# Three sequences in one expert table, the fourth through all experts: a routed block on one core

## The chip, the cores and the metric

The kernel runs on one core of a Trainium2 chip. The metric is the device time of one execution in microseconds (us). The engines are named as in the profile: PE (TensorE matmuls; PEld its weight loads), DVE (VectorE), ACT (ScalarE), POOL (GpSimd) and SP (SyncE, which here only issues DMAs). Each engine runs its own instructions in the order in which they were laid down.

## The reference

The input is four sequences (b = 0 to 3) of 512 tokens with 128 features. A modulated layer norm, a convolution block with a gate and a residual come first, per sequence. Then each token goes to 8 of 160 small experts:

```python
logits = x @ router_w.T + expert_bias[None, :]
probs = jax.nn.sigmoid(logits)
top_w, top_idx = jax.lax.top_k(probs, TOP_K)
top_w = top_w / (jnp.sum(top_w, axis=-1, keepdims=True) + 1e-09)
top_w = top_w * ROUTED_SCALE
combine = combine.at[jnp.arange(T)[:, None], top_idx].set(top_w)
h1 = jax.nn.silu(jnp.einsum('th,eih->eti', x, w_gate))
h1w = h1 * combine.T[:, :, None]
routed = jnp.einsum('eti,ehi->th', h1w, w_down)
shared = jax.nn.silu(x @ w_gate_shared.T) @ w_down_shared.T
```

The output is x + gb * (routed + shared), where gb is a modulation per sequence. All is float32.

## The kernel before, in words

**Sequences.** `sequence(b)` (L281) is a generator with five parts; the loop at L954 interleaves the parts of neighbouring sequences. It computes the convolution block, the router's probabilities `prob` (L418), the 8 largest (`top`, L439), and from running counts a table row for each choice (`ranks`, `keys`, `slot_in`, L456 to L512). `shared` is the shared expert.

**Two halves.** Sequences 0 and 1 share one table and one pass of the experts, 2 and 3 another. A table has 64 rows for each expert and 56 (`NOV`, L50) spare blocks of 128 rows for experts that get more: 17,408 rows of 512 bytes. `clear(i)` (L149) writes zeros into a whole table beforehand, on SP's queue.

**Dispatch.** `dispatch(b)` (L627) scatters the tokens into the table: 32 indirect DMAs on POOL (L661), each after a small copy `pick` (L659). Between them it runs other POOL work, step by step: `residual_sums`, and `places(b)` (L592), which computes the weights of each choice.

**Experts.** `experts(s)` (L676) walks over its table in groups of 1,024 rows: 10 groups of own rows (`own_blocks`, 16 experts each, weights resident) and 7 of spare blocks (`overflow_blocks`, whose weights `ow` are loaded by 8 DMAs of SP, L740, at addresses that it reads at run time). A group is: load `xg` (L685), 8 transposes into `px` (L691), two copies to `xs` (L692), matmuls into `ph` (L714 or L750), Silu (L719 or L755), matmuls into `py` (L724 or L760), two copies to `yg` (L702, L703), and a store into the result table (L704). `xg`, `xs`, `yg` and `ow` have two buffers each.

**Combine.** `combine(b)` (L769) gathers the 8 result rows of each token: 32 indirect DMAs on POOL (L800). For b < 2, POOL also multiplies each gathered row by its weight (L777) and DVE adds up (L786); for b of 2 and 3, DVE does both (L782, L784).

**Fallback.** If the spare blocks don't suffice, `dense(b)` (L811) under `tc.If` (L981) computes a sequence through all 160 experts. In this data that branch isn't taken.

**Order.** Each buffer has a tag (`own(b, ...)`: one buffer for odd and one for even sequences; `bank(i, ...)`, `ps_x`, `ps_y`: two PSUM banks each). A planner lays down each engine's order ahead of the run, by the order of the program and by its own view of when things are ready; `behind(b, what)` pins an instruction behind another of its engine. The end of the program is:

```python
    dispatch(B - 1)
    for _ in places(B - 1, nc.vector):
        pass
    w_pairs += [weights(g) for g in (NGO - 2, NGO - 1)]
    experts(0)
    outs = [combine(b) for b in range(2)]
    experts(1)
    outs += [combine(b) for b in range(2, B)]
```

Of the kernel before, what the change touches and what calls it, by code (L numbers as in the profile page):

```python
# [39 lines left out]
P = 128  # L41
# [8 lines left out]
NOV = 56  # L50
# [42 lines left out]
def adaln_block(  # L93
# [48 lines left out]
    tables, results = [], []  # L142
    for i in range(2):
        t = dram.tile([ROWS, D], F32, tag=f"table{i}", name=f"table{i}")
        tables.append(t)
        t = dram.tile([ROWS, D], F32, tag=f"result{i}", name=f"result{i}")
        results.append(t)

    def clear(i):  # L149
        nc.sync.dma_start(  # L150
            tables[i].rearrange("(p i r) f -> p i (r f)", p=P, r=4),
            zero.unsqueeze(1).to_broadcast([P, ROWS // P // 4, 4 * D]),
        )

    clear(0)
    for b in range(2, B):
        nc.sync.dma_start(x_sb[b], rows_of(x_rows, b))
    clear(1)
# [30 lines left out]

    mark = const.tile([P, P], BF16, name="mark")  # L190
# [15 lines left out]
    short = const.tile([1, 2], I32, name="short")  # L206
# [69 lines left out]
    ready, halves, keep, last, scattered, residual, found, shared = ({} for _ in range(8))  # L276

    def behind(b, what):
        return tc.issue_after(last[what, b].ins) if (what, b) in last else nullcontext()

    def sequence(b):  # L281
# [153 lines left out]
        chosen = own(b, [P, NT, E], BF16, "out_wg", "chosen")  # L435
        for half in range(2):
            for t in (2 * half, 2 * half + 1):

                nc.vector.max(out=top[:, t, :], in_=prob[:, t, :])  # L439
                nc.vector.match_replace(  # L440
                    out=repl[:, t, :], in_to_replace=top[:, t, :], in_values=prob[:, t, :], imm_value=-1.0
                )
            at = ds(2 * half, 2)
            nc.vector.tensor_scalar(chosen[:, at, :], repl[:, at, :], 0.0, None, ALU.is_lt)
        h2 = own(b, [P, NT, D], F32, "h2", "h2")
# [15 lines left out]
        new, away = ranks[:, 4, :].bitcast(I32), ranks[:, 5 - b % 2, :]  # L461

        cum = ranks[:, 5, :] if b % 2 else own(b, [P, E], F32, "cum", "cum")
        if b % 2 == 0:
            nc.vector.tensor_single_scalar(new, n, P - 1.0 - BLK, ALU.add)
        else:
            was = halves[b // 2]
            nc.vector.scalar_tensor_tensor(new, n, P - 1.0 - BLK, was["cap"], ALU.add, ALU.subtract)
        nc.vector.tensor_single_scalar(new, new, 7, ALU.logical_shift_right)
        nc.vector.tensor_tensor_scan(  # L470
            cum, ones_e, new, 0.0 if b % 2 == 0 else was["cum"][:, E - 1 : E], ALU.mult, ALU.add
        )
        nc.vector.tensor_sub(away, cum, new)
        if b % 2:
            nc.vector.tensor_sub(away, away, was["new"])
        nc.vector.scalar_tensor_tensor(away, away, float(P), far, ALU.mult, ALU.add)
        if b % 2:
            nc.vector.tensor_sub(away, away, was["moved"])
        key_at = key_own if b % 2 == 0 else was["key"]
# [4 lines left out]
        for half in range(2):  # L484
# [15 lines left out]
            if b % 2 == 0:  # L500
                nc.vector.scalar_tensor_tensor(k1, rank, MARK + BLK, both(away), ALU.is_ge, ALU.mult)
            else:
                nc.vector.scalar_tensor_tensor(k1, rank, -MARK - BLK, both(was["cap"]), ALU.add, ALU.is_ge)
# [5 lines left out]
        ikey = work.tile([P, NT, TOPK], I32, tag="ikey", name=f"ikey{b}", bufs=B)  # L509
# [6 lines left out]
        with behind(b, "slots"):  # L516

            if b % 2 == 0:
                newf = own(b, [P, E], F32, "newf", "newf")
                nc.vector.tensor_copy(newf, new)  # L520
                moved = own(b, [P, E], F32, "moved", "moved")
                nc.vector.scalar_tensor_tensor(moved, newf, 1.0, away, ALU.is_ge, ALU.mult)
                cap = own(b, [P, E], F32, "cap", "cap")
                nc.vector.scalar_tensor_tensor(cap, newf, float(P), n, ALU.mult, ALU.subtract)
                key1 = own(b, [P, E], F32, "key1", "key1")
                nc.vector.tensor_add(key1, key_own, moved)
                nc.vector.tensor_add(key1, key1, n)
                halves[b // 2] = {"cap": cap, "cum": cum, "new": newf, "moved": moved, "key": key1}
            else:

                junk = ranks[0:NOV, 0, :]
                eo = own(b, [NOV, 2], F32, "eo", "eo")
                for i, c in enumerate((was["cum"], cum)):
                    nc.vector.scalar_tensor_tensor(
                        junk, c[0:NOV, :], iota_q[0:NOV], ones_e[0:NOV, :], ALU.is_le, ALU.mult,
                        accum_out=eo[:, i : i + 1],
                    )
                nc.vector.scalar_tensor_tensor(eo[:, 0:1], eo[:, 0:1], float(E), eo[:, 0:1], ALU.is_lt, ALU.mult)
                nc.vector.tensor_add(eo[:, 0:1], eo[:, 0:1], eo[:, 1:2])
                peo = bank(b, f"peo{b}")  # L540
                nc.tensor.matmul(peo[0:1, 0:NOV], eo[:, 0:1], ident[0:NOV, 0:NOV], start=True, stop=True)
                eo_row = work.tile([1, NOV], I32, tag="eo_row", name=f"eo_row{b}", bufs=2)
                nc.vector.tensor_scalar_min(eo_row, peo[0:1, 0:NOV], float(E - 1))
                nc.vector.tensor_single_scalar(
                    short[:, b // 2 : b // 2 + 1], cum[0:1, E - 1 : E], float(NOV), ALU.is_gt
                )
                halves[b // 2]["eo_row"] = eo_row
# [3 lines left out]
        row = work.tile([P, NT, TOPK], U32, tag="row", name=f"row{b}", bufs=B)  # L551
        idx = work.tile([P, NT, TOPK], U32, tag="idx", name=f"idx{b}", bufs=B)
# [5 lines left out]

        ph = bank(b, f"phs{b}")
# [209 lines left out]
    def combine(b):  # L769
# [37 lines left out]
        while pending:  # L807
            finish(*pending.pop(0))
# [241 lines left out]
```

## Time and profile before

| | us |
|---|---|
| median of 3 runs (lowest, highest) | 522.31 (520.89, 526.49) |
| the profiled execution: time | 523.86 |
| its span, first to last instruction | 522.2 |
| PE busy (2,532 matmuls) | 305.5 (59%) |
| POOL busy | 358.0 (69%) |
| DVE busy | 221.1 (42%) |
| ACT busy | 152.5 (29%) |
| moved by DMA | 98.57 MB |

Spans are counted from the first instruction. A PE that is busy need not be at its peak: matmuls are pipelined and their ends are modelled. A float32 matmul is two MATMUL records (two passes), a transpose or a bf16 matmul is one.

### The profile page before, as it was taken

Reading aid. Unit: us, or ns where it says so; the run is one execution under the profiler, and the core shown is the slowest. Engines: PE = TensorE matmul, PEld = TensorE weight load, DVE = VectorE, ACT = ScalarE, POOL = GpSimd, SP = SyncE. Lnnn points to the kernel's source line nnn. Section 1 sums busy time; section 2 is a strip of 40 time slices with the busy share of each in tenths; the row PEclk is TensorE's granted clock in tenths of the full one; section 3 lists DMA queues with packets and bytes.
Section 4 is the critical chain, followed back from the end, with each engine's and each line's share of the span. In section 5 each row is a group of like instructions: output and inputs, shape, how many; then the busy total and the mean of one; then the engine's idle time right before and its main releaser. Section 6 shows DMA issues by size and latency. Waiting matters only on the chain.

```text
span 522.2 us, 7733 instructions
## 1 busy us (share of the span) xinstructions
PE 305.5 (59%) x2532; PEld 208.2 (40%) x2532; DVE 221.1 (42%) x708; ACT 152.5 (29%) x298; POOL 358.0 (69%) x520
## 2 busy tenths in 40 slices
PE   5996997895569687676865834667777630000000
PEld 3644443443333466555643633545665520000000
DVE  7286785892586256562621401111332004333331
ACT  3463645351614152121210221314545520000000
POOL 8616168988888888568878038888898018777771
PEclk9999997798569997696885766657878985555555
DMA  8999994025411455395886583426999921212111
GB/s 273 409 394 409 324 419 196 30 80 153 137 35 66 146 185 176 118 288 170 284 291 212 184 260 126 167 82 211 300 302 299 335 103 45 70 50 75 50 56 36
DMA packets 50368, 98.57 MB, mean 189 GB/s; under 512 B 7633, under 2 KB 26130, under 8 KB 48914
## 3 DMA queue, kind: packets, MB, share of 16 engines
q1 hardware_dynamic: 36144, 61.20, 34.3%
q0 software_dynamic: 8192, 16.79, 10.4%
q10 hardware_dynamic: 5986, 20.03, 10.3%
q8 instruction: 22, 0.36, 0.3%
q14 instruction: 24, 0.20, 0.1%
HBM read 50.54 MB, written 47.45 MB: 188 GB/s over the span
## 4 chain that ended last, share of the span: by engine, by line
POOL 26%; PE 25%; issue 22%; DMA 10%; DVE 9%; ACT 3%; SPq 2%; POOLq 1%; ACTq 0%; DVEq 0%
POOL table L661 11%; POOL yk L800 10%; PE px L691 5%; PE py L724 4%; PE ph L714 4%; DMA xg<-table 3%; PE ph L750 2%; POOL pick L659 2%; PE py L760 2%; PE ph L323 2%; SPq L740 2%; DMA ow<-in_w_ov 2%; DMA yk<-result,row 2%; DMA mat<-in_mats 2%; DVE s L370 1%
## 5 line engine op out<-in xcount | busy, mean ns | idle before, releaser
L800 POOL DMA_INDIRECT yk<-result,row x128 | 124.9, 976 | 72.7 <-issue 51.8
L661 POOL DMA_INDIRECT table<-h,pick x116 | 118.8, 1024 | 33.5 <-POOL pick L659 17.5
L691 PE MATMUL px<-ident,xg 128*128 128x128 f32 x272 | 52.0, 337 | 26.3 <-issue 13.3
L691 PEld LDWEIGHTS px<-ident,xg 128*128 128x128 f32 x272 | 38.1, 171 | 34.7 <-issue 24.6
L724 PE MATMUL py<-w_g,h 64*64 64x128 f32 x640 | 32.1, 348 | 21.7 <-issue 16.2
L714 PE MATMUL ph<-xs,w_g 128*64 128x64 f32 x640 | 38.3, 262 | 9.6 <-issue 9.0
L784 DVE SCALAR_TENSOR_TENSOR out_sb<-yk,idx,out_sb 128x128 f32<-128x128 f32 x56 | 19.9, 355 | 48.9 <-DMA yk<-result,row 47.2
L659 POOL COPY pick<-slot_in 128x1 uint32<-128x1 uint32 x116 | 26.1, 226 | 19.9 <-DVE slot_in L512 19.5
L786 DVE TENSOR_TENSOR out_sb<-out_sb,yk 128x128 f32<-128x128 f32 x48 | 15.0, 319 | 57.1 <-POOL yk L777 47.6
L702 ACT COPY yg<-py 128x512 f32<-128x512 f32 x34 | 19.9, 585 | 65.9 <-PE py L724 21.9
L714 PEld LDWEIGHTS ph<-xs,w_g 128*64 128x64 f32 x640 | 31.2, 169 | 17.7 <-issue 15.1
L692 DVE COPY xs<-px 128x512 f32<-128x512 f32 x34 | 22.5, 683 | 36.2 <-PE px L691 18.0
L724 PEld LDWEIGHTS py<-w_g,h 64*64 64x64 f32 x640 | 25.1, 175 | 27.9 <-issue 19.8
L760 PE MATMUL py<-ow,h 64*128 64x128 f32 x224 | 19.8, 327 | 20.6 <-issue 11.1
L365 PE MATMUL pc<-val,dia 128*128 128x512 f32 x64 | 28.1, 592 | 0.0
L777 POOL TENSOR_TENSOR yk<-yk,idx 128x128 f32<-128x128 f32 x64 | 25.9, 412 | 1.0
L760 PEld LDWEIGHTS py<-ow,h 64*128 64x128 f32 x224 | 16.7, 224 | 23.9 <-issue 12.4
L370 DVE SCALAR_TENSOR_TENSOR s<-val,vec,s 128x512 f32<-128x512 f32 x32 | 25.6, 799 | 0.6
L719 ACT ACTIVATE h<-ph 128x512 f32<-128x512 f32 x20 | 11.9, 597 | 44.8 <-remote 20.9
L692 ACT COPY xs<-px 128x512 f32<-128x512 f32 x34 | 19.2, 587 | 16.4 <-DMA ow<-in_w_ov 8.2
L703 DVE COPY yg<-py 128x512 f32<-128x512 f32 x17 | 11.7, 687 | 27.1 <-remote 9.9
L323 PE MATMUL ph<-hf,in_wn 128*128 128x512 f32 x32 | 22.4, 844 | 0.8 <-issue 0.7
(247 smaller groups left out, 558.8 us busy)
## 6 DMA issues: line engine op xcount, KB each, us to landing
table<-early SPq DMA_DIRECT2D x2, 8704.0 KB
xg<-table SPq DMA_DIRECT2D x34, 512.0 KB
result<-yg ACTq DMA_DIRECT2D x34, 512.0 KB
ow<-in_w_ov SPq DMA_DIRECT2D x112, 96.0 KB
w_g<-in_w_gd SPq DMA_DIRECT2D x10, 1024.0 KB
yk<-result,row POOLq DMA_INDIRECT x128
table<-h,pick POOLq DMA_INDIRECT x116
x<-in_x SPq DMA_DIRECT2D x4, 256.0 KB
```

The costliest lines, as they stand in the source:

```text
L323: nc.tensor.matmul(ph, in_wn[:, ts(o, P)], hf, start=True, stop=True)
L365: nc.tensor.matmul(pc, dia[:, k, :], val[:, 0, k : k + L], start=(k == 0), stop=(k == npe - 1))
L370: last["conv", b] = nc.vector.scalar_tensor_tensor(s[:, 1, :], val[:, 1, k : k + L], v("sym_k", KS + k), s[:, 1, :], ALU.mult, ALU.add)
L659: nc.gpsimd.tensor_copy(at, slot_in[:, t, k : k + 1])
L661: last["scatter", b] = nc.gpsimd.indirect_dma_start(out=tables[b // 2], out_offset=bass.IndirectOffsetOnAxis(ap=at, axis=0), in_=h2[:, t, ...
L691: nc.tensor.transpose(px[:, c, :], xg[:, 4 * half + c, :], ident)
L692: (nc.scalar.copy if s else nc.vector.tensor_copy)(xs[:, ds(4 * half, 4), :], px)
L714: nc.tensor.matmul(ph[ds((r ^ (j & 1)) * INTER, INTER), j, :], w[:, j, 0, ds(r * INTER, INTER)], xs[:, :, ds(16 * j + 8 * r, 8)], start=Tr ...
L724: nc.tensor.matmul(py[j & 1][ds(r * BLK, BLK), j // 2, :], h[at, j, :], w[at, j, 1, :], start=True, stop=True)
L760: nc.tensor.matmul(py[r][:, c, :], h[at, c, :], ow[at, c, r, ds(r * INTER, D)], start=True, stop=True)
L777: last["weight", b] = nc.gpsimd.tensor_mul(row, row, wk[:, t, k : k + 1].to_broadcast([P, D]))
L800: last["fetch", b] = nc.gpsimd.indirect_dma_start(out=yk[:, k, :], out_offset=None, in_=results[b // 2], in_offset=bass.IndirectOffsetOnAx ...
```

## The change

`NOV` goes from 56 to 96, and there is one table, one result and one clearing, of 22,528 rows. Sequences 0, 1 and 2 (`NS` = 3) are dispatched into it, with running state carried over three sequences instead of two. There is one pass `experts()` of 10 own and 12 spare groups, and three combines of 32 gathers each, which start when the whole pass has been stored.

Sequence 3 is not dispatched. Its part of `sequence` ends after the router: the masked probabilities (`repl`, `top`) go to `dense_in`. `dense(3, ...)` becomes a generator: it splits the weights of the choices into three bf16 parts, transposes them (`combT`), and then does 80 iterations, one per pair of experts. An iteration is two matmuls of 64 output rows into `ph`, one bf16 matmul with a selection matrix (`sel`) that spreads the weights of the two experts over 128 rows (`pb`), Silu on ACT, a multiplication on DVE, and one matmul that adds into `acc`. The program text interleaves one iteration with each gather. `selectors()` builds `sel` on POOL. The gathered rows `yk` now live in the buffers of `xg` and `yg`, and the buffers of `dense` are those of the sequences. In `experts()`, DVE does both copies to `xs` and the second one to `yg`.

```diff
-NOV = 56
+NS = B - 1
+NOV = 96
...
+        if b == NS:
+            dense_in[b] = (h2f, repl, top)
+            yield
+            shared_expert(b, h2f, x1)
+            ready[b] = (None, None, x1)
+            yield
+            return
...
-                for other in ((0,), (1, 2))[b - 2]:
+                for other in range(b):
                     yield from places(other, nc.gpsimd)
...
-                (nc.scalar.copy if s else nc.vector.tensor_copy)(xs[:, ds(4 * half, 4), :], px)
+                nc.vector.tensor_copy(xs[:, ds(4 * half, 4), :], px)
...
-            if s and g % 2:
+            if g % 2:
...
-            (nc.scalar.copy if s else nc.vector.tensor_copy)(at(yg, 1), py[1])
+            nc.vector.tensor_copy(at(yg, 1), py[1])
...
+        done = 0
         for g in range(NGO):
             own_blocks(g)
-            if g >= NGO - NOV // GP:
-                overflow_blocks(g - NGO + NOV // GP)
+            while done < (g + 1) * (NOV // GP) // NGO:
+                overflow_blocks(done)
+                done += 1
...
-            yk = own(t, [P, TOPK, D], F32, "s" if t < 2 else "gate", f"yk{b}_{t}")
+            yk = moe.tile([P, TOPK, D], F32, tag="xg" if t < 2 else "yg", name=f"yk{b}_{t}")
...
+                yield
...
-        return out_sb
+        nc.sync.dma_start(rows_of(out_rows, b), out_sb)
...
+    def selectors():
+        tiles_of = []
+        for i in range(2):
+            sel = own(i, [3 * ECH, JCH // 2, P], BF16, "mod", "sel")
+            nc.gpsimd.memset(sel, 0.0)
...
+                    nc.gpsimd.affine_select(
+                        out=at, in_=at, compare_op=ALU.not_equal, fill=1.0,
...
+    def dense(b, h2f, comb, top):
...
             pb = ps_y.tile([P, 512], F32, tag="y", name=f"pb_d{b}_{j}")
-            nc.tensor.matmul(pb, sel[:, j % JCH, :], combT[:, j // JCH, :], start=True, stop=True)
-            hs = moe.tile([P, L], F32, tag="xs", name=f"hs_d{b}_{j}")
+            c, i = j // JCH, j % JCH
+            nc.tensor.matmul(
+                pb, sel[2 * i // JCH][:, i % (JCH // 2), :], combT[c // 2][:, c % 2, :], start=True, stop=True
+            )
+            hs = own(0, [P, L], F32, ("fm", "low")[j % 2], f"hs_d{b}_{j}")
             nc.scalar.activation(hs, ph, AF.Silu)
             nc.vector.tensor_mul(hs, hs, pb)
             nc.tensor.matmul(acc, w[:, j % GP, 1, :], hs, start=(j == 0), stop=(j == NPAIR - 1))
+            yield
...
-    dispatch(B - 1)
-    for _ in places(B - 1, nc.vector):
+    for b in range(2, NS):
+        for _ in places(b, nc.vector):
+            pass
+    w_pairs += [weights(g) for g in (NGO - 2, NGO - 1)]
+    for _ in shared_sums(NS):
         pass
-    w_pairs += [weights(g) for g in (NGO - 2, NGO - 1)]
-    experts(0)
-    outs = [combine(b) for b in range(2)]
-    experts(1)
-    outs += [combine(b) for b in range(2, B)]
...
+    sel = selectors()
+    experts()
+    last_one = dense(NS, *dense_in[NS])
+    next(last_one)
+    for b in range(NS):
+        for _ in combine(b):
+            next(last_one, None)
+    for _ in last_one:
+        pass
```

`shared_expert` and `shared_sums` hold code that stood in `sequence` and `dispatch`. In the text of `combine`, each `yield` lets one dense iteration be laid down.

## The prediction

> **What bounds the kernel now.** I read the page first (busy shares, the slices, the costliest groups), then the timelines of POOL, SP and PE stage by stage, because each stage has another limit.
>
> ```profile
> PE   5996997895569687676865834667777630000000
> POOL 8616168988888888568878038888898018777771
> PEclk9999997798569997696885766657878985555555
> ...
> L800 POOL DMA_INDIRECT yk<-result,row x128 | 124.9, 976 | 72.7 <-issue 51.8 <-DMA result<-yg 19.9 <-DMA yk<-result,row 0.9
> L661 POOL DMA_INDIRECT table<-h,pick x116 | 118.8, 1024 | 33.5 <-POOL pick L659 17.5 <-issue 14.0 <-DMA w_g<-in_w_gd 0.7
> L777 POOL TENSOR_TENSOR yk<-yk,idx 128x128 f32<-128x128 f32 x64 | 25.9, 412 | 1.0
> ```
>
> Slices are 13.05 us. POOL is nearly full from 68 to 287 us (scatters) and from 307 to the end (gathers); PE is empty for the last 90 us at a granted clock of 0.5. Scatters, experts and gathers lie behind one another, so I follow three seams:
>
> ```profile
> 223.64 0.27 POOL L659 COPY pick<-slot_in 128x1 uint32<-128x1 uint32 x1 [6.29 <-DVE slot_in L512]
> ...
> 233.85 0.98 POOL L661 DMA_INDIRECT table<-h,pick  x1 [0.28 <-issue]
> ...
> 286.28 0.98 POOL L661 DMA_INDIRECT table<-h,pick  x1 [0.28 <-issue]
> ...
> 423.94 0.33 ACTq L704 DMA_DIRECT2D result<-yg  x1
> 428.25 0.94 POOL L800 DMA_INDIRECT yk<-result,row  x1 [22.50 <-issue]
> ...
> 510.89 0.94 POOL L800 DMA_INDIRECT yk<-result,row  x1 [0.30 <-issue]
> ```
>
> Counted in order, scatter 64 starts at 175.38 us, scatter 96 at 233.85 and scatter 128 at 286.28. Before scatter 90 POOL stood 6.29 us for `slot_in` of sequence 3: its first `pick` copy had been laid down among sequence 2's scatters. The last store of the second pass is issued at 423.94; the gathers of sequences 2 and 3 wait for it and run from 428.25 to 511.83; the span ends at 522.2.
>
> For PE, one full-clock stretch and one of long matmuls (start, duration):
>
> ```profile
> 407.63 1.06 PE L691 MATMUL px<-ident,xg 128*128 128x128 f32 x8 [1.24 <-DMA xg<-table]
> 408.62 1.10 PE L724 MATMUL py<-w_g,h 64*64 64x128 f32 x32
> 409.66 1.09 PE L750 MATMUL ph<-xs,ow 128*64 128x128 f32 x16
> 410.68 1.09 PE L691 MATMUL px<-ident,xg 128*128 128x128 f32 x8
> ...
> 159.85 7.89 PE L365 MATMUL pc<-val,dia 128*128 128x512 f32 x18
> ```
>
> A full-width pass of 512 columns takes 7.89/18 = 0.438 us, so one of 128 takes 0.110. Sixteen half-width passes (L750) one behind another would take 1.75 us; they take 1.02 from start to start, as two side by side (0.88) and 0.15 more.
>
> **The change, part by part.**
>
> *Front, to the last scatter.* The fourth dispatch goes (235.1 to 287.3). Scatter 96 ends at 233.85 + 0.98 = 234.8, less the 6.3 us for `slot_in` of sequence 3, which POOL no longer needs: 228.5. Four `hit` products of `places(1)` move into this dispatch (a step takes 1.78 us with one, 1.45 without: +1.3), two `h2` halves of sequence 3 leave it (0.72 each, -1.4): nothing. `slot_in` of sequence 2 was ready at 161.1 and its first scatter came at 176.67, so the extra running state on DVE (some ten operations of 0.3 us) has 15 us of cover; uncovered, 3 us. The cleared table shrinks from 17.4 to 11.5 MB (`table<-early` x2 of 8.7 MB), behind a first scatter that waited 0.7 us for a DMA: nothing. `selectors()` on POOL: 12 selects of 640 elements at the rate of L186 (128 in 0.293 us) and two fills, about 20 us, in POOL's idle time during the pass; +20 if laid down before a scatter.
>
> *Pass of the experts.* From the end of scatter 64 (176.4) to the first transpose of its table (181.17) are 4.8 us, so the new pass starts at 228.5 + 4.8 = 233.3. A pair of an own and a spare group took (421.64 - 361.36)/6 = 10.05 us in the second pass (starts of L760), and its DMA share was 0.89. Ten pairs and two extra spare groups at half a pair: 110.5 us. Bounds: 91 (the last stretch, 404.6 to 417.6, moved 336 GB/s; a pair moves 2.77 MB, 8.2 us) and 148 (the mean of the whole second pass, 114.5/17 = 6.74 us a group, times 22). I take 110.5, as no gathers run beside it now, but dense iterations do. Last store at 343.8, first gather 4.3 us later (423.94 to 428.25): 348.1.
>
> *Gathers.* 96 instead of 64 lie behind the pass. Sequences 0 and 1: 306.98 to 405.76, 98.8 us, and five weighings that ran later (2.1). Sequence 2: (83.6 - 2.1)/64 = 1.273 each, 40.7 us. Together 141.6: 489.7. The end, from the last gather to the span's end, is 10.4: 500.1.
>
> *Gathers beside DVE.* The dense product (`hs`, 0.7 us of DVE, 80 times) now runs beside the gathers. Scatters, issued beside a busy DVE, took 1.024 us on average against 0.976 for gathers: 96 x 0.048 = 4.6 us. Bounds 0 and 14 (single scatters at 110 to 113 us took 1.34 and 1.57 while DVE was 0.95 busy). I take 4.6: 504.7. [...]
>
> *The dense sequence.* One iteration on PE: `ph`, four half-width passes of 512 as two side by side, 2 x 0.438; `pb`, one bf16 pass (160 columns start 0.07 us apart at L489 and L493, so 512 take 0.22); `acc`, 2 x 0.438; two changes of array shape, 0.15 to 0.17 each (above). That is 2.3 us, 183 for 80. Bounds: 1.97 without the changes, 3.17 with the halves of `ph` one behind the other. ACT (0.6) and DVE (0.7) fit below it. [...]
>
> Where do 183 us go? Sequence 3's probabilities were ready at 196.6, some 5 us late because DVE stood before `xs` of the first pass (4.6 us idle after `x`, 177.7). With about 10 us of preparation on DVE and PE dense starts near 208. Until 233.3: 11 iterations. In the pass PE has 110.5 - 22 x 3.6 = 31 us free, at most 13 iterations; but the order is laid down beforehand and their priority is lowest: I take 4. Beside the gathers 141.6/2.3 = 61. Left over: 4, that is 9.2 us behind the last gather. Bounds 0 and 16 or more (first rival).
>
> *Sum.* 233.3 + 110.5 + 4.3 + 141.6 + 10.4 + 4.6 + 9.2 = 513.9 us of span. The profiled time is 1.7 above its span, and 1.55 above the median: 514 us.
>
> **Rivals.**
>
> 1. *Dense work is left behind the gathers (slower).* DVE's order holds both the products of dense and the sums of the gathers. If the planner counts the halves of `ph` one behind the other (3.17), it puts 45 iterations beside the gathers and 8 before; the rest follows the last sum, however early PE was free. Sixteen left over at 2.3 are 37 us: 542. For it: orders that don't fit the run show twice in this trace, the 6.29 us above, and gathers of sequence 2 queued ahead of the last weighings of sequence 1, which held POOL from 405.8 to 428.3. Against: how the planner counts isn't seen. It decides from about ten left over (527).
> 2. *The pass is slower.* At 6.74 us a group it takes 148 us, 38 more, less the 9 us of dense left over, for more would fit into it: 543. For it: both passes had stretches in which PE waited for "issue" (13.3 us before L691, 16.2 before L724). Against: from 361 us on they are gone. It decides from 5.6 us a group.
> 3. *All of dense is hidden and the pass runs at the DMA's rate (faster).* 91 us for the pass, no rest, nothing from DVE: 514 - 19.5 - 9.2 - 4.6 = 481; with half of the gain in the pass, 488. For it: PE's clock, 0.74 and 0.85 in the passes, should rise to 1 with dense work between. Against: SP alone needs nearly 5 us for the 8 weight loads of a spare group.
> 4. *The change doesn't do what it says.* With more than 96 spare blocks the fallback runs for three sequences, 3 x 183 us more: above 1,050. Counted with the reference's own choices, three sequences need 81.
>
> **How the numbers follow.** What can be told from no change here is about 1%, 517.1 to 527.5. My sum with its smaller bounds spans 498 to 528: 0.40, of which 0.24 faster, 0.13 the same, 0.03 slower. Rival 3: 0.18, faster. Rival 1: 0.24, of which 0.02 the same. Rival 2: 0.13, slower. Rival 4 and others not seen: 0.05, slower. Faster 0.42, the same 0.15, slower 0.43: a near-even case, and the sum decides the time. The range leaves out the quick end of rival 3 (0.07) and, above, the longer tails of rivals 1 and 2 and all of rival 4 (0.13): 484 to 552; the forecast's own is 498 to 528.
>
> **What would show it.** Right: about 96 scatters ending near 228 us without a wait for `slot_in` of a fourth sequence; the first L691 near 233; the last store near 344; gathers of sequences 0 and 1 every 1.6 us and of 2 every 1.27; PE at clock 1.0 from about 210 to 490 with dense iterations 2.3 us apart; few of them after the last gather. Wrong: dense matmuls going on for 20 us or more behind the last gather with DVE idle before them (rival 1); px groups further apart than 5.6 us (rival 2); half-width passes of 512 columns 0.438 apart rather than in pairs, which would make every iteration 3.17 us; scatters that wait for the selectors. If the last gather comes before 470 us, my pass is too long.

## The result, and the profile after

The changed kernel takes 559.78 us (median of 4 runs, 555.69 to 560.55) against 521.6 us for the kernel before (4 runs, 519.65 to 526.49): 1.070 times as long, with a 95% interval of 1.061 to 1.079. I had predicted 514 us, 484 to 552, with chances of 0.42 for faster and 0.43 for slower; the direction of the 514 us and its size are both wrong.

The page of the changed kernel (slices of 13.94 us, span 557.7 us, profiled execution 559.48 us), with the groups of the gathers and of the dense matmuls:

```profile
PE   5988977987934700039768669899999999986994
...
POOL 8535288888999888820000000088889888871000
PEclk9999996897985555559879798999999999997998
...
L822 POOL DMA_INDIRECT yk<-result,row x96 | 94.9, 988 | 140.6 <-PE ph_d L897 120.0
...
L906 PE MATMUL acc_d<-hs_d,w_g 128*128 128x512 f32 x160 | 90.9, 650 | 3.5 <-DVE hs_d L905 2.5
L897 PE MATMUL ph_d<-h2f,w_g 128*64 128x512 f32 x320 | 86.8, 623 | 6.4 <-ACT hs_d L904 5.7
```

PE is no longer empty at the end, as it was before. It is empty earlier, between 195 and 246 us (the zeros in its row, clock 0.5), and it goes on for 45 us after POOL has stopped. The timeline of the changed kernel gives the seams (start, duration, engine, line, what, and in brackets the idle time before it and what ended it):

```profile
169.81 3.12 POOL L860 TENSOR_SCALAR_AFFINE_SELECT sel<-sel 120x640 bf16<-120x640 bf16 x4
...
201.68 0.42 DVE L636 TENSOR_REDUCE idx<-hit 128x32 f32<-128x256 f32 x1 [11.33 <-POOL hit L633]
...
212.85 0.49 DVE L879 CAST parts_d<-repl 128x640 bf16<-128x640 f32 x1
...
240.22 0.98 POOL L682 DMA_INDIRECT table<-h,pick  x1 [0.28 <-POOL pick L680]
...
246.08 3.02 PE L711 MATMUL px<-ident,xg 128*128 128x128 f32 x12 [53.48 <-DMA xg<-table]
...
348.56 0.39 PE L886 MATMUL pt_d<-ident,parts_d 128*120 128x128 bf16 x4
...
355.57 2.85 PE L897 MATMUL ph_d<-h2f,w_g 128*64 128x512 f32 x12 [0.67 <-ACT yg L722]
...
361.20 1.00 POOL L822 DMA_INDIRECT yk<-result,row  x1 [120.00 <-PE ph_d L897]
...
502.90 0.94 POOL L822 DMA_INDIRECT yk<-result,row  x1 [0.30 <-issue]
...
515.17 1.08 PE L897 MATMUL ph_d<-h2f,w_g 128*64 128x512 f32 x4
...
517.45 1.08 PE L897 MATMUL ph_d<-h2f,w_g 128*64 128x512 f32 x4
...
548.38 1.12 PE L906 MATMUL acc_d<-hs_d,w_g 128*128 128x512 f32 x2 [0.33 <-DVE hs_d L905]
```

Scatter 96 comes at 240.2 and the pass starts at 246.1; the last store of the pass is issued at 355.8; the gathers run from 361.2 to 503.8; the last dense matmul ends at 549.5; the span ends at 557.7. The dense sequence had its `parts_d` at 212.85, but its first transpose on PE (`pt_d`) came at 348.56 and its first `ph_d` at 355.57, when the pass was done. How the passes of `acc_d` (two per iteration) lie in the four stages, in the windows of that tile (window, length, PE busy and count, then weight loads, ACT, clock, DMA share, GB/s):

```profile
196.00:246.00 50.00, 0.00 (x0) 0.00 (x0) 0.00 (x0) 0.50 0.15 53
246.00:361.00 115.00, 1.48 (x3) 0.59 (x4) 0.00 (x0) 0.87 0.78 263
361.00:504.00 143.00, 67.17 (x120) 17.54 (x118) 0.00 (x0) 1.00 0.17 48
504.00:549.00 45.00, 21.72 (x38) 5.94 (x38) 0.00 (x0) 0.93 0.03 8
```

None of 80 iterations before the pass, one or two at its end, 60 beside the gathers, 19 behind them. Against my sum:

| Part | Predicted | Measured | Difference |
|---|---|---|---|
| Front, to the first transpose of the pass | 233.3 | 246.1 | +12.8 |
| Pass, to the issue of its last store | 110.5 | 109.7 | -0.8 |
| From there to the first gather | 4.3 | 5.4 | +1.1 |
| Gathers, with what DVE costs them | 146.2 | 142.6 | -3.6 |
| Dense work behind them, and the end | 19.6 | 53.9 | +34.3 |
| Span | 513.9 | 557.7 | +43.8 |

The two large rows were the subject of the experiments.

### The profile page after: what moved, and what is told of

Read it like the earlier page. It is cut to its first block, busy times and chain, and to the rows that moved or that the text cites. A ratio compares the mean times of both kernels' runs of the same rounds, so it can differ in the third digit from the quotient of the medians.

```text
span 557.7 us, 7083 instructions
## 1 busy us (share of the span) xinstructions
PE 422.3 (76%) x2292; PEld 201.4 (36%) x2292; DVE 273.4 (49%) x737; ACT 158.4 (28%) x303; POOL 302.9 (54%) x433
## 4 chain that ended last, share of the span: by engine, by line
PE 32%; POOL 28%; DVE 13%; DMA 10%; issue 9%; ACT 4%; SPq 2%; another core or an unknown queue 2%; POOLq 0%; ACTq 0%; DVEq 0%
POOL yk L822 11%; POOL table L682 8%; PE ph_d L897 6%; DMA xg<-table 6%; PE acc_d L906 6%; POOL yk L799 4%; PE px L711 3%; PE pc L381 2%; PE py L744 2%; DVE s L386 2%; PE ph L339 2%; POOL pick L680 2%; DMA mat<-in_mats 2%; SPq L760 1%
## 5 line engine op out<-in xcount | busy, mean ns | idle before, releaser
L822 POOL DMA_INDIRECT yk<-result,row x96 | 94.9, 988 | 140.6 <-PE ph_d L897 120.0
L682 POOL DMA_INDIRECT table<-h,pick x84 | 88.8, 1058 | 22.1 <-POOL pick L680 12.8
L906 PE MATMUL acc_d<-hs_d,w_g 128*128 128x512 f32 x160 | 90.9, 650 | 3.5 <-DVE hs_d L905 2.5
L897 PE MATMUL ph_d<-h2f,w_g 128*64 128x512 f32 x320 | 86.8, 623 | 6.4 <-ACT hs_d L904 5.7
L904 ACT ACTIVATE hs_d<-ph_d 128x512 f32<-128x512 f32 x80 | 47.9, 598 | 144.2 <-PE acc_d L906 110.8
L711 PE MATMUL px<-ident,xg 128*128 128x128 f32 x176 | 32.9, 329 | 70.7 <-DMA xg<-table 70.6
L905 DVE TENSOR_TENSOR hs_d<-hs_d,pb_d 128x512 f32<-128x512 f32 x80 | 54.5, 682 | 42.9 <-ACT hs_d L904 36.7
L906 PEld LDWEIGHTS acc_d<-hs_d,w_g 128*128 128x128 f32 x160 | 24.1, 189 | 69.7 <-issue 35.8
L897 PEld LDWEIGHTS ph_d<-h2f,w_g 128*64 128x64 f32 x320 | 16.0, 135 | 57.6 <-issue 49.6
L900 PE MATMUL pb_d<-combT_d,sel 120*128 120x512 bf16 x80 | 30.4, 382 | 0.0
L680 POOL COPY pick<-slot_in 128x1 uint32<-128x1 uint32 x84 | 21.1, 252 | 12.2 <-DVE slot_in L539 12.1
```

Of the source, the lines that this page charges most:

```text
L680: nc.gpsimd.tensor_copy(at, slot_in[:, t, k : k + 1])
L682: last["scatter", b] = nc.gpsimd.indirect_dma_start(out=table, out_offset=bass.IndirectOffsetOnAxis(ap=at, axis=0), in_=h2[:, t, :], in_of ...
L711: nc.tensor.transpose(px[:, c, :], xg[:, 4 * half + c, :], ident)
L822: last["fetch", b] = nc.gpsimd.indirect_dma_start(out=yk[:, k, :], out_offset=None, in_=result, in_offset=bass.IndirectOffsetOnAxis(ap=slo ...
L897: nc.tensor.matmul(ph[at, :], w[:, j % GP, 0, ds(r * INTER, INTER)], h2f, start=True, stop=True)
L900: nc.tensor.matmul(pb, sel[2 * i // JCH][:, i % (JCH // 2), :], combT[c // 2][:, c % 2, :], start=True, stop=True)
```

## The experiments

The theory (theory 1): dense takes its PSUM tiles from the tags that the pass uses. `pt_d` lies with `px`, `ph_d` with the odd groups' `py`, `pb_d` with the even groups' `py`, `acc_d` with `ph`. Buffers of a tag are handed out in the order of the text, and dense's text stands behind `experts()`; so its first matmul waits for the last tiles of the pass, however early its data is there and however idle PE is. The rivals: its low priority in the planner (2), data that is not ready (3), and DVE's order, which holds up the iterations beside the gathers (4, my first rival as I had written it).

Not all runs were on one chip, and the kernel before takes another time on each (473 to 522 us). So times of changed kernels are compared where they ran on the same chip (where two chips are compared, the text says so): experiments 1 to 4 (kernel before: 512.5 us), 5 to 8 (474.0), 9, 10, 13 and 14 (473.0), 11 and 12 (512.7), 15 and 16 (513.1).

**1. Dense's text before the pass.**

```diff
     sel = selectors()
+    last_one = dense(NS, *dense_in[NS])
+    for _ in range(14):
+        next(last_one)
     experts()
-    last_one = dense(NS, *dense_in[NS])
-    next(last_one)
```

> Edit: the text of the dense sequence, its preparation and the first 13 of its 80 iterations, stands before the pass of the experts instead of behind it; everything else as in the changed kernel (559.8 us). Theory 1 (buffers): the PSUM tags of dense are those of the pass and are handed out in the order of the text, so dense could not start before the last groups of the pass; now its first matmul comes near 214 us (parts_d were ready at 212.85), 13 iterations of 2.28 us run until about 246, the pass starts within 2 us of 246.1, and only 19 - 13 = 6 iterations follow the last gather: 559.8 - 13 x 2.28 = 530 us, range 524 to 538. Theory 3 (data): something that dense reads is not ready before the end of the pass; PE then stands before the pass and the time is the same or longer, above 556. Theory 4 (pace): the iterations beside the gathers are held by the order of DVE, so fewer in front does not help: 550 to 560, with gaps of more than 2.28 us between the iterations beside the gathers. The theory of priorities (2) also expects about 530 here and is told apart by the run in which only the priority changes.

Measured: 527.66 us, 1.032 of the kernel before (1.026 to 1.038). The timeline of PE (first lines of dense, then the pass and the last `acc_d`):

```profile
215.55 1.78 PE L886 MATMUL pt_d<-ident,parts_d 128*120 128x128 bf16 x12 [14.55 <-DVE parts_d L879]
...
224.19 1.08 PE L897 MATMUL ph_d<-h2f,w_g 128*64 128x512 f32 x4
...
226.47 1.08 PE L897 MATMUL ph_d<-h2f,w_g 128*64 128x512 f32 x4
...
248.28 3.01 PE L711 MATMUL px<-ident,xg 128*128 128x128 f32 x12 [3.44 <-DMA xg<-table]
...
519.40 1.13 PE L906 MATMUL acc_d<-hs_d,w_g 128*128 128x512 f32 x2 [0.33 <-DVE hs_d L905]
```

The transposes now wait for their data alone (`parts_d`), and iterations follow 2.28 us apart until the pass starts, about when it did. The last gather is issued at 506.2, and what is left of dense after it ends at 520.5: six iterations instead of 19. On the same chip the kernel of experiment 3, which behaves as the changed kernel, took 556.24; the 28.6 us between them are 13 iterations of 2.2 us. Theories 3 and 4 fall.

**2. Ten iterations inside the pass as well.**

```diff
         for g in range(NGO):
             own_blocks(g)
+            next(last_one)
```

> Edit: as the run before, and one more iteration of dense in the text behind each of the ten groups of own blocks, so that 23 of 80 stand before the end of the pass. Theory 1: PE has 110 - 22 x 3.6 = 31 us free in the pass, so ten iterations (23 us) fit; 57 are left for the 142.6 us of the gathers (62 fit), none behind them: the last gather near 504, the end 10.4 later, 514 to 518 us with the time around the span. If each iteration prolongs the pass by its 2.28 us (PE or one PSUM buffer of the ph tag, held by acc, as the bound of the pass): 23 us later, 538. Theory 4 (pace): 540 to 560.

Measured: 532.92 us, 5 more than experiment 1 on that chip. Dense now ends (509.3) before the gathers do (522.3), as wanted; but from the first `px` to the first gather it is 135.1 us instead of 116.2. That is 1.9 us for each of the ten iterations in the pass, nearly the 2.28 that one costs behind the gathers, and they save only the six that were left. The free PE time that I had counted inside the pass (31 us) could not be had at this place.

**3. Only the priority.**

```diff
     last_one = dense(NS, *dense_in[NS])
-    next(last_one)
+    with tc.high_priority():
+        next(last_one)
+        for _ in range(14):
+            next(last_one)
```

> Edit: the text of dense stays behind the pass; only the planner's priority of its preparation and its first 14 iterations is set to the highest. Theory 1 (buffers are handed out in the order of the text): nothing moves, the first ph_d still comes after the last px of the pass (near 355 us), 557 to 562 us. Theory 2 (low priority): PE takes the iterations from about 214 us on as soon as they are ready, 524 to 538 us.

Measured: 556.24 us. The pass and the first `ph_d`, in PE's timeline:

```profile
247.35 3.01 PE L711 MATMUL px<-ident,xg 128*128 128x128 f32 x12 [53.54 <-DMA xg<-table]
...
357.39 2.85 PE L897 MATMUL ph_d<-h2f,w_g 128*64 128x512 f32 x12 [0.67 <-ACT yg L722]
```

With the highest priority, dense still starts behind the pass and PE stands 53.5 us before it. Theory 2 falls. (Experiment 11 tells the turn at the buffers from the mere place in the text.)

**4. The selectors behind the last scatter.**

```diff
-    sel = selectors()
+    with behind(NS - 1, "scatter"):
+        sel = selectors()
```

> Edit: the two fills and twelve selects of the selectors are queued on GpSimd behind the last scatter instead of among the scatters; all else as in the changed kernel. If the selectors delayed the front by their own 12.2 us: scatter 96 starts near 228 instead of 240.2, the pass near 234, and the whole kernel ends 12 us earlier: 547.6 us, range 545 to 551, as the product needs them only after the pass. If the scatters would have waited for something else (slots of the third sequence, DVE) anyway: 554 to 561.

Measured: 550.65 us (548.26 to 553.65), 5.6 less than experiment 3 on the same chip (552.10 to 559.74). In POOL's timeline the last scatter and the first gather:

```profile
229.36 0.97 POOL L682 DMA_INDIRECT table<-h,pick  x1 [0.28 <-POOL pick L680]
...
354.65 1.02 POOL L822 DMA_INDIRECT yk<-result,row  x1 [113.14 <-PE ph_d L897]
```

The front is 12.1 us shorter (241.45 to 229.36 us): the fills and selects had indeed been laid among the scatters. But from the first `px` to the first gather this run took 119.4 us, experiment 3 115.4. That stretch took 109 to 119 us in the ten profiles of this study in which the pass has all its buffers and no dense iterations among its groups, so those 4 us lie within what it varies; why it varies is open.

**5. The dense product left out.** 78 of the 80 iterations are missing, so the fourth sequence lacks most of its routed sum.

```diff
-        for j in range(NPAIR):
+        for j in (0, NPAIR - 1):
```

> Left out: 78 of the 80 iterations of the dense sequence (its output is then incomplete); preparation, the other three sequences and the changed kernel's order stay. It measures what dense costs at the end and what it costs the gathers beside it. Theory 1: the front and the pass are unchanged (first gather near 361), the end comes 10.4 us after the last gather, so about 45 us of the changed kernel's time go: span 509 to 514 (time 511 to 516 on a chip where the changed kernel takes 559). My step 'gathers beside DVE' (4.6 us): the 96 gathers then take 138 us; if the product on DVE costs the gathers nothing, 141 to 143. A theory by which the pass itself was slowed by the change would show the same pass here and no more than 45 us gained.

Measured: 512.61 us, span 512.8. The chip is another than in the first comparison, but up to the last gather the profile is nearly the same: first `px` at 246.7 (246.1), first gather at 361.8 (361.2), last gather's end at 504.8 (503.8). Behind it 8.0 us are left instead of 53.9. So some 46 us of the changed kernel are dense work behind the gathers. The group of the gathers without the product beside them:

```profile
L822 POOL DMA_INDIRECT yk<-result,row x96 | 95.3, 993 | 140.8 <-DMA result<-yg 120.2
```

0.993 us each, against 0.988 with the product: it costs the gathers nothing that shows, and my 4.6 us for it were wrong.

**6 to 8. Small selectors, an earlier preparation.** A selector repeats each one-hot column 64 times. In experiment 6 the columns are stored once, made at the start, and repeated by a stride of 0 as the stationary operand is read (`dense`'s text stands before the pass, with 13 iterations, as in experiment 1):

```diff
-            sel = own(i, [3 * ECH, JCH // 2, P], BF16, "mod", "sel")
+            sel = const.tile([3 * ECH, JCH // 2, 2], BF16, name=f"sel{i}")
...
+            for e in range(2):
+                nc.tensor.matmul(
+                    pb[ds(e * INTER, INTER), :],
+                    sel[2 * i // JCH][:, i % (JCH // 2), e : e + 1].to_broadcast([3 * ECH, INTER]),
+                    combT[c // 2][:, c % 2, :], start=True, stop=True,
+                )
```

> Edit: the selectors lose their 64-fold repeated columns (20 one-hot columns each, made at the start), and pb takes its stationary operand with a stride of 0 over 64 columns, in two half-width passes; dense starts before the pass with 13 iterations as in the first run. Nothing of the selectors is left among the scatters: scatter 96 near 229 (as in the run with late selectors). The preparation is not earlier (parts_d near 212 or, as DVE waits for products of GpSimd that come 11 us earlier now, near 202). Theory 1: if parts are ready near 202, 13 iterations fit before the pass at 235 and the end comes 11 us before that of the first run: 517 us; if near 212, nine fit and four hold the pass up: 526. If the stride of 0 makes the weight load or the pass slower, the distance of iterations beside the gathers rises above 2.28 us.

Measured: 513.73 us. The last scatter comes at 230.3, the pass starts at 236.2, the first gather is at 346.8. The first iterations behind the preparation run at 204 us. With both repairs together the kernel is 39 to 46 us below the changed kernel (552.3 and 559.8 us), but those were measured on other chips.

Experiment 7 moves `dense`'s text before the third dispatch, with 15 iterations, puts `parts_d` into the buffers that the selectors had, and queues the sums of GpSimd's products (the `idx<-hit` that held DVE for 11.33 us above) behind the preparation:

```diff
-        parts = own(1, [P, NT, NCH, 3, ECH], BF16, "val", f"parts_d{b}")
+        parts = [own(i, [P, NT, 2, 3, ECH], BF16, "mod", f"parts_d{b}") for i in range(2)]
...
-        with behind(NS - 1, "slots"):
+        with behind(NS, "prep"):
             nc.vector.tensor_reduce(wk, hit, AX.X, ALU.add)
```

> Edit: as the run before, and dense's text moves before the third dispatch, its parts lie in the buffers that the selectors no longer need (instead of the buffer of the products of GpSimd), and DVE's sums of those products are queued behind the preparation. Theory 1, extended to SBUF buffers: probabilities are ready at 190 us, the preparation takes 8 to 10, so iterations run from about 199; 15 of them until the pass at 235. First gather near 351, last near 493, 3 iterations and 10 us behind it: 505 to 513 us. If the preparation still waits for products of GpSimd (theory 3), the iterations start after 205 and hold the pass up: 515 to 525.

Measured: 517.15 us, a miss. The preparation did come early (iterations from 197 us), and 7.3 us of dense were left behind the last gather instead of 11.8; but only 13 of the 15 iterations ended before the pass, at 227.6. PE then stood 8.3 us for the first `px`, and the last products of the other two came behind it, from 238.0 to 241.6, in the pass. From the first `px` to the first gather it was 120.9 us instead of 110.7.

Experiment 8 adds three iterations in the pass (behind the own blocks of every third group):

> Edit: as the run before, with three more iterations inside the pass (behind the own blocks of groups 1, 4 and 7). In the second run each of ten iterations in the pass made it 1.7 us longer. Then three cost 5 us in the pass and take 6.8 us from behind the gathers: within 3 us of the run before. If they are free in the pass (PE idle there), 4 to 7 us faster; if one held buffer of the ph tag was what made the pass longer, as much as with ten: 10 us slower.

Measured: 519.07 us. The pass grew by another 8.3 us, 2.8 per iteration. In the pass's own turn for buffers, iterations were free neither here nor in experiment 2.

**9. Nineteen iterations before the pass.**

```diff
-            for _ in range(16):
+            for _ in range(20):
                 next(last_one)
+            last["turned", NS] = last["acc", NS]
```

(`last["acc", NS]` is the latest `acc_d` matmul; the line queues the first `px` on PE behind it.)

> Edit: as the run with the early preparation, with 19 iterations instead of 15 before the pass, and the first transposes of the pass queued on PE behind the last of them. There PE stood from about 227 to 236 us before the pass, so four more iterations cost nothing or 2 us of start. 80 - 19 = 61 iterations are left for the gathers (62 fit), none behind them: first gather 349 to 357 as the pass takes 101 to 109, last gather 491 to 499, end 10 later: 505 to 511 us with the time around the span, against 517 with four less in front. If the iterations behind the last gather stay all the same (held by DVE's order), 513 to 518.

Measured: 506.70 us (504.16 to 508.07). The seams in the timeline:

```profile
237.59 2.27 PE L910 MATMUL acc_d<-hs_d,w_g 128*128 128x512 f32 x4
239.70 1.04 PE L711 MATMUL px<-ident,xg 128*128 128x128 f32 x8
...
490.78 0.94 POOL L822 DMA_INDIRECT yk<-result,row  x1 [0.30 <-issue]
...
493.14 1.13 PE L910 MATMUL acc_d<-hs_d,w_g 128*128 128x512 f32 x2 [1.40 <-DVE hs_d L909]
```

PE runs from dense into the pass without a gap, and dense ends 2.5 us after the last gather.

**10. Shorter gathers on top.** GpSimd's weighing of sequences 0 and 1 goes into DVE's sums, as sequence 2 has it:

```diff
-            if b >= 2 and k == 0:
+            if k == 0:
                 nc.vector.tensor_scalar_mul(acc, yk[:, 0, :], wk[:, t, 0:1])
-            elif b >= 2:
+            else:
```

> Edit: as the run before, and GpSimd's weighing of the rows of sequences 0 and 1 goes into DVE's sums, as sequence 2 has it. Each of those 64 gathers then comes every 1.27 us instead of 1.6: 20 us less, the gathers take 122. But 61 iterations need 139 us, so 17 us of dense lie behind the last gather: only 3 to 5 us faster than the run before if PE is the bound (500 to 508). If DVE can't keep pace (hs and the sums in one queue), the iterations are more than 2.28 us apart and the run is not faster.

Measured: 505.77 us, where I had expected a gain of 3 to 5; the four executions took 497.89 to 506.44, so whether there is a small gain is unclear. The gathers end at 469.7, 22 us earlier than in experiment 9, yet dense ends at 495.5 where it ended at 494.3: from the first gather on, PE's 61 iterations need 145 us in both.

**11 and 12. Tags of its own.** Dense's text and priority stay behind the pass; its PSUM tiles come from two banks of their own, taken from the tags of `px` and of the pass's `ph`:

```diff
-    ps_m = [ctx.enter_context(tc.tile_pool(name=f"ps_m{i}", bufs=2, space=PSUM)) for i in range(2)]
-    ps_x = ctx.enter_context(tc.tile_pool(name="ps_x", bufs=2, space=PSUM))
+    ps_m = [ctx.enter_context(tc.tile_pool(name=f"ps_m{i}", bufs=1 + i, space=PSUM)) for i in range(2)]
+    ps_x = ctx.enter_context(tc.tile_pool(name="ps_x", bufs=1, space=PSUM))
+    ps_d = ctx.enter_context(tc.tile_pool(name="ps_d", bufs=1, space=PSUM))
...
-            ph = bank(1, f"ph_d{b}_{j}")
+            ph = ps_d.tile([P, 512], F32, tag="d", name=f"ph_d{b}_{j}")
```

> Edit: dense's text and priority stay as in the changed kernel, behind the pass, but its PSUM tiles come from two banks of their own (one for acc, one in turn for the transposes, ph and pb); in exchange the tags of px and of the pass's ph have one buffer instead of two. Theory 1: with tags of its own nothing of the pass holds dense up. Its first transposes wait for parts_d alone (213 us or a little later, as the front may be longer with fewer buffers), some iterations run before the first px, more between the groups of the pass, and 25 or so of 80 are done when the gathers begin. With one bank for ph and pb in turn an iteration takes about 3.4 us (1.0 ph, 0.6 ACT, 0.3 pb, 0.7 DVE and waits), so 40 to 55 beside and behind the gathers need 140 to 190 us and the whole time is 530 to 600, no measure of anything. Theory that only the place in the text or the planner's ranking decides, whatever the tags: the first ph_d comes after the last px, as in the changed kernel.

> Edit: as the run before, the tags of px and of the pass's ph have one buffer instead of two, but dense still takes its tiles from the pass's tags (control). Theory 1: the first ph_d comes after the last px of the pass, none of 80 iterations before the pass, 18 or more behind the gathers; 560 to 600 us, as front and pass lose buffers. If the smaller number of buffers alone lets dense start early, its first ph_d comes before the pass here too.

Measured: 614.47 us with the tags of its own, 577.50 for the control. Where dense begins, in PE's timeline of the first:

```profile
219.88 0.68 PE L887 MATMUL pt_d<-ident,parts_d 128*120 128x128 bf16 x4 [12.72 <-DVE parts_d L880]
...
224.38 1.97 PE L898 MATMUL ph_d<-h2f,w_g 128*64 128x512 f32 x4 [0.52 <-DVE combT_d L890]
...
252.42 1.11 PE L712 MATMUL px<-ident,xg 128*128 128x128 f32 x4 [4.45 <-DMA xg<-table]
```

and of the control:

```profile
253.09 1.12 PE L711 MATMUL px<-ident,xg 128*128 128x128 f32 x4 [46.76 <-DMA xg<-table]
...
375.95 1.94 PE L897 MATMUL ph_d<-h2f,w_g 128*64 128x512 f32 x8
```

With the same text, dense starts 33 us before the pass when the tags are its own, and 7 us behind the last `px` when they are shared. That settles theory 1. The times are no measure of a version: with one bank in turn an iteration waits for ACT and DVE (4.0 us apart, where I had expected 3.4), and 84 us of dense lie behind the last gather. One thing more is to be seen: from the first `px` to the first gather it is 128.6 us in the first run with 24 iterations in it, and 128.7 in the control with one. In this one pair of profiles, iterations inside the pass cost nothing with tags of their own, which they did in experiments 2 and 8, where they stood in the pass's own queue for buffers. But this pass is 13 us longer than with all buffers (115.4 in experiment 3), so it also has more room.

**13 and 14. Both kernels again, on one chip.**

> The kernel before, unchanged, with a profile. In three comparisons it took 521.6, 512.5 and 474.0 us, while kernels of the changed kind kept their fronts and passes within 1 to 2 per cent. If something of the chip (its clock, its transfers) is faster where the kernel before takes 474, all stages of it are shorter by the same share, and the changed kernel too; if one stage of the kernel before is unsteady (the second pass with its gathers beside it, 109 to 115 us here), the stage before 286 us and the gathers behind the pass stay the same and 10 to 48 us lie in the passes alone.

> The changed kernel, unchanged, beside the kernel before on this chip: 555 to 561 us, whatever the kernel before takes, if its stages are as steady as the four profiles of its kind show (last scatter 240 to 242, pass 102 to 106, gathers 142).

Measured: the kernel before 472.5 us, the changed one 552.29, 1.163 of the kernel before (1.155 to 1.171). The changed kernel's front, pass and gathers are within 3 us of what they were; the kernel before is 50 us shorter. Its first pass starts at 181.3 us, as it did (181.2), and the difference lies in its two passes. From first `px` to last store they took 121.6 and 114.5 us in the profile that I predicted from, and take 94.8 and 85.5 here. PE's waits differ. In the first profile of the kernel before, between 181 and 424 us (waiting for what: us in total, times, longest):

```profile
PE py L724 <- issue: 16.2, 6, 5.7
PE px L691 <- issue: 13.3, 10, 7.6
PE px L691 <- DMA xg<-table: 11.8, 6, 4.2
PE py L760 <- issue: 11.1, 5, 5.4
...
PE ph L714 <- issue: 9.0, 24, 0.7
```

The same view of the same kernel on this chip:

```profile
PE px L691 <- DMA xg<-table: 37.6, 17, 10.7
PE py L760 <- ACT h L755: 5.9, 5, 1.5
PE px L691 <- DVE xs L692: 4.3, 2, 3.9
```

PE's waits for "issue" add up to 51.2 us in the whole of the first profile and to none here, where transfers hold up the passes most. That is one half of it: in the passes PE also has 164.6 us of work in the first profile and 135.1 here, at a granted clock of 0.78 and 0.76 against 0.83 to 0.94 (six stretches of 21 to 30 us in the passes). Whether the waits lower the clock, or one cause brings both, is not shown. In the changed kernel the waits for "issue" are 3.8 us and none.

**15 and 16. Experiment 9 again, and the kernel before beside it.**

> The kernel with 19 iterations before the pass, unchanged, measured once more. If its time hardly depends on the chip (its pass runs without GpSimd beside it, and PE's waits for issue were 3.8 us at most in kernels of its kind): 504 to 514 us, which is 0.97 to 1.0 of the kernel before on a chip where that takes 512 to 522, and 1.07 again on one where it takes 473. If the waits come back with dense beside the gathers: 520 to 550.

> The kernel before, unchanged, for its profile on this chip: where it takes 512 to 522 us, PE's waits for issue add up to 35 to 55 us and lie in the two passes; where it takes 473, there are none.

Measured, on another chip: 513.18 us, 1.002 of the kernel before (513.14; 0.998 to 1.005), and a profile of the kernel before of 511.73 us. Its waits of PE between 181 and 424 us:

```profile
PE px L691 <- DMA xg<-table: 21.8, 7, 7.7
PE py L724 <- issue: 20.6, 6, 7.1
PE py L760 <- issue: 9.0, 4, 4.6
```

The waits for "issue" are there again (40.7 us in the whole profile; 5.1 in that of experiment 9 on this chip), and so is the time above 510 us. Experiment 9 moved by 6.5 us from one chip to the other, the kernel before by 40.

## Why the prediction was wrong

*The step that failed* is "Until 233.3: 11 iterations. In the pass ... I take 4." I had asked when the data was ready and when PE was free, and both answers were nearly right (208 against 213 us; PE empty until 246). I had not asked which buffers dense takes and who gets them first. No iteration ran before the pass and hardly one in it; 19 were left instead of 4. Experiment 1 moved the text and nothing else and got 28.6 us back; experiment 3 moved the priority and got nothing. Experiment 11 left the text and gave dense tags of its own, and it started before the pass, which it did not in the control with as few buffers: theory 1.

*The selectors.* "In POOL's idle time during the pass" was wrong, and the other end that I had given ("+20 if laid down before a scatter") came true, at a smaller price: 12.2 us of work, 12.1 us of front (experiment 4). With the sum otherwise as it was, this alone makes 526 us of my 514, and no gain is left.

*The first rival* named the right consequence, dense work behind the gathers, at 542 us, but not the cause. Its own counts (45 iterations beside the gathers, 8 before) would have left 27 or, with 4 in the pass, 23, not sixteen. The sign that I had given for it, 20 us or more of dense work behind the last gather, came true too, so it could not tell the two causes apart. I had put it down to DVE's order; the iterations beside the gathers ran at 2.33 us on average (380 to 440 us) with PE busy for 59.2 of these 60 us, so DVE did not hold them.

*What held.* The iteration: 2.28 us measured, 2.3 predicted. Its passes alone add up to 1.97 by my rows; the 0.31 us left over fit my estimate of 0.15 to 0.17 for each of two changes of array shape, but no run takes these apart. The pass: 109.7 against 110.5, partly by luck, as from first `px` to last store it took 106 to 114 us in the ten profiles named above, and I had counted four dense iterations in it. The gathers: 142.6 against 141.6. The removed wait for `slot_in` and the moved `hit` products: with the selectors out of the way the last scatter came at 229.4, where I had 227.5 for its start.

*Smaller slips.* Besides the 4.6 us for DVE beside the gathers (nothing in experiment 5), three readings were off without moving the result: seven weighings ran late and not five (under 1 us); half of the gain in the pass in rival 3 makes 490, not 488; and the waits for "issue" were not gone from 361 us on, as 6.4 of the 51.2 us come later.

*What the base hid.* Experiment 9 takes 506.7 and 513.2 us, close to my 514. That is partly chance, as it does more than repair the failed steps: its preparation is earlier, and 19 iterations stand before the pass where I had 11 there and 4 in it. Yet it is 1.072 of the kernel before (1.066 to 1.078) where that takes 473.0, and equal to it where that takes 513.1. The kernel before lets its second pass run beside the gathers of sequences 0 and 1. Where its passes run at the pace of the transfers (experiment 13: a DMA share of 0.86 to 0.96 from 285 to 366 us), POOL gathers nearly without a gap from 281.1 to 463.7 us and that pass costs nothing. The ends of its row of gathers in the profile of experiment 13, right behind the last scatter (first line):

```profile
279.80 0.98 POOL L661 DMA_INDIRECT table<-h,pick  x1 [0.28 <-DMA ow<-in_w_ov]
281.08 1.00 POOL L800 DMA_INDIRECT yk<-result,row  x1 [0.30 <-issue]
...
462.77 0.94 POOL L800 DMA_INDIRECT yk<-result,row  x1 [0.30 <-issue]
```

With one table POOL stands idle for the whole pass (116 us from the last scatter to the first gather in experiment 9). Where PE has its waits for "issue", the old passes are long enough to hold the gathers up (the 22.5 us of POOL before 428.25 in the profile that I used), and it is those waits that the merged pass does without (5.1 us in the whole of experiment 9 on the chip where the kernel before has 40.7). Nothing of GpSimd runs beside it, but that this is the reason is not shown. I had named the waits as evidence that the new pass could be slow (rival 2); they were a cost of the old passes. On the chip of the first comparison (521.6 us) experiment 9 was not tried; none of the versions tried beats the kernel before where it was measured.

## What to carry to other kernels

When independent work is to fill an idle engine, look up which buffers it takes and where its text stands among their other users; with shared tags it started here after the last of them, and a higher priority didn't help. Small helpers (fills, selects) belong to an engine's queue like everything else: fix their place behind what is urgent, or make them so small that it doesn't matter. Before counting a stall as a gain, ask whether it belongs to the kernel or to the run: merging two overlapped passes into one gives up the overlap for good, and what it removes may not be there on another chip.

## What the runs showed of the hardware

- One program, unchanged, took 521.6 us on one chip and 472.5 on another. In the slower profile PE waits for nothing that the profile shows, up to 7.6 us at a time or a fraction of a microsecond between short matmuls: a group of 32 passes of `ph` took 10.4 us, 341.5 to 351.9, where the changed kernel's take 1.15. GpSimd was at work in 74% of this waiting time and in 70% of the two passes as a whole, and the longest wait, 301.9 to 309.5, lies mostly where it stood still. So the waits are not tied to GpSimd's work by this trace, and what PE lacks there is not shown.
- After 5.7 us without work PE ran the next iteration at half speed (`ph_d` 1.97 us instead of 1.08, `acc_d` 2.08 instead of 1.12) from 506.43 to 510.2, and then at full speed; the granted clock was 0.50 from 506 to 510 us and 1.00 from 514 to 549. The lines of the changed kernel:

```profile
506.43 1.97 PE L897 MATMUL ph_d<-h2f,w_g 128*64 128x512 f32 x4 [5.68 <-ACT hs_d L904]
508.33 2.08 PE L906 MATMUL acc_d<-hs_d,w_g 128*128 128x512 f32 x2
510.20 0.47 PE L900 MATMUL pb_d<-combT_d,sel 120*128 120x512 bf16 x1
510.60 1.08 PE L897 MATMUL ph_d<-h2f,w_g 128*64 128x512 f32 x4
```

- A stationary operand read with a stride of 0 over 64 columns costs nothing that can be seen: in experiment 9, before the pass, iterations are 2.25 us apart with it and 2.28 without (experiment 1). `pb_d` became two half-width passes at the same time, so the two effects are not told apart.
